# Which gathers SyncE fetches, and how the last step of a spiking recurrence is cut into pieces

## The chip, the cores and the metric

The kernel runs on one core of one Trainium2 chip. The metric is the time of one execution on the device, in microseconds. Beside it there is a profile of one execution, taken by the hardware profiler; its times are counted from the start of that execution.

The core's engines work side by side and meet at semaphores. TensorE (PE in the profile) multiplies matrices and transposes, VectorE (DVE) and ScalarE (ACT) work elementwise, GpSimd (POOL) here issues the gathers, and SyncE (SP) issues plain transfers. Transfers run on DMA engines of their own.

## The reference

A table of 100001 items with 128 values each is read for 1024 users with 50 items each. From the running mean of a user's items, normalised over the users at every step, a spiking neuron is driven; the mean of its spikes is multiplied with the whole table.

```python
emb = emb_table.at[0].set(0.0)
e = emb[seq]                                   # 1024 users x 50 steps x 128
prefix = jnp.cumsum(e, axis=1)
denom = jnp.minimum(t_idx[None, :], lengths[:, None])
uF = prefix / denom[:, :, None]
mean = uF.mean(axis=0)                         # over the users
var = uF.var(axis=0)
y = (uF - mean) * lax.rsqrt(var + BN_EPS) * gamma + beta
x_seq = jnp.moveaxis(y, 1, 0)

def step(v, x):
    v = v + (x - v) / TAU                      # TAU = 2
    spike = atan_spike(v - V_TH)               # 1 where v >= 1
    v = v - spike * V_TH
    return (v, spike)

_, spikes = lax.scan(step, v0, x_seq)          # 50 steps, one after the other
uF_out = spikes.mean(axis=0)
scores = uF_out @ emb.T                        # 1024 x 100001
```

## The kernel before

The kernel has two stages. The first is the recurrence: for every step, GpSimd gathers 1024 rows of the table, 128 rows (one "column block" of users) at a time; TensorE transposes them, adding onto the running sums `pre` in PSUM; VectorE makes `uF`, its statistics, the scale `a`, and the new `v`; ScalarE applies scale and bias. `negv` holds spike minus v of the step before, so that v = x/2 + v_old/2 - spike/2 is one instruction. The spikes are counted by TensorE in `sums`.

Some of the gathers, four of 400, are not made by GpSimd. SyncE reads the item numbers into registers and starts one transfer of 512 bytes for each row, after it has started the transfer of the first 36 blocks of the table.

```python
        for g in range(AHEAD):
            fetch(group(g), g * GROUP, GROUP)
# ...
        aside = {}
        for t0, many in ((T - 6, 4),):
            for t in range(t0, t0 + many):
                aside[t] = once.tile([P, P], F32, tag=f"aside{t}", name=f"aside_{t}")
            for p in range(P):
                _, items = nc.values_load_multi_w_load_instructions(
                    idx[p : p + 1, 0, t0 : t0 + many],
                    engines=[mybir.EngineType.SP],
                    min_val=0,
                    max_val=N - 1,
                    skip_runtime_bounds_check_because="items are rows of the table; the transfer checks its own bounds",
                )
                for j, item in enumerate(items):
                    nc.sync.dma_start(out=aside[t0 + j][p : p + 1, :], in_=table[bass.ds(item, 1), :])

        es = {}

        def gather(t):
            es[t] = gp.tile([P, B], F32, tag="e", name=f"e_{t}")
            for n in range(t in aside, NB):
                nc.gpsimd.indirect_dma_start(
                    out=es[t][:, n * P : (n + 1) * P],
                    out_offset=None,
                    in_=table,
                    in_offset=bass.IndirectOffsetOnAxis(ap=idx[:, n, t : t + 1].bitcast(U32), axis=0),
                )
```

`fetch(r, q, n)` starts the transfer of `n` blocks of 1024 table rows (512 KB each).

The body of a step. The last step (49) differs: its spikes and `negv` come first, and after the statistics TensorE does transpositions into `warm`, whose results nobody reads, until the products begin.

```python
        for t in range(T):
            last = t == T - 1
            if t + 1 < T:
                gather(t + 1)
            e = es.pop(t)
            if last:
                s = lp.tile([P, B], BF16, tag="s", name=f"s_{t - 1}")
                nc.vector.tensor_single_scalar(s, v, V_TH, ALU.is_ge)
                nc.vector.tensor_tensor(negv, s, v, ALU.subtract)
            uF = up.tile([P, B], F32, tag="uF", name=f"uF_{t}")
            bs = sp.tile([P, B // BANK, 6], F32, tag="bs", name=f"bs_{t}")
            for h, cs in enumerate(halves):
                for k in range(0, BANK, P):
                    nc.tensor.matmul(
                        pre[h][:, k : k + P],
                        lhsT=aside[t] if h == k == 0 and t in aside else e[:, h * BANK + k : h * BANK + k + P],
                        rhs=ident,
                        start=False,
                        stop=last,
                        is_transpose=True,
                        skip_group_check=True,
                    )
                nc.vector.scalar_tensor_tensor(uF[:, cs], rlen[:, cs], 1.0 / (t + 1), pre[h], ALU.max, ALU.mult)
                nc.vector.bn_stats(bs[:, h, :], uF[:, cs])
            if not last:
                correct(t + 1, l)
            else:

                counted(t - 1, s)
                count = once.tile([P, B], F32, tag="zT", name="count")
                for h, cs in enumerate(halves):
                    nc.scalar.copy(count[:, cs], sums[h])
            mv = sp.tile([P, 2], F32, tag="mv", name=f"mv_{t}")
            nc.vector.bn_aggr(mv, bs.rearrange("p h s -> p (h s)"))


            r = sp.tile([P, 1], F32, tag="r", name=f"r_{t}")
            nc.scalar.activation(r, mv[:, 1:2], AF.Sqrt, bias=eps)
            nc.scalar.activation(uF, uF, AF.Identity, bias=mv[:, 0:1], scale=-1.0)


            if t and not last:
                s = lp.tile([P, B], BF16, tag="s", name=f"s_{t - 1}")
                nc.vector.tensor_single_scalar(s, v, V_TH, ALU.is_ge)
                counted(t - 1, s)

            nc.vector.reciprocal(r, r)
            q = sp.tile([P, 1], F32, tag="q", name=f"q_{t}")
            nc.vector.tensor_mul(q, r, r)
            nc.vector.scalar_tensor_tensor(q, mv[:, 1:2], BN_EPS, q, ALU.add, ALU.mult)
            nc.vector.tensor_scalar(q, q, -0.5, 1.5, ALU.mult, ALU.add)
            a = sp.tile([P, 1], F32, tag="a", name=f"a_{t}")
            nc.vector.tensor_scalar(a, q, r, hgb[:, 0:1], ALU.mult, ALU.mult)


            def x(vt, cs):
                nc.scalar.activation(vt, uF[:, cs], AF.Identity, bias=hgb[:, 1:2], scale=a)

            def step(vt, cs):
                nc.vector.scalar_tensor_tensor(vt, negv[:, cs], -0.5, vt, ALU.mult, ALU.add)

            if not last:
                vt = vp.tile([P, B], F32, tag=f"v{t % 2}", name=f"v_{t}")
                x(vt, whole)
                if t:
                    nc.vector.tensor_tensor(negv, s, v, ALU.subtract)
                step(vt, whole)
                v = vt
                if t + 2 < T:
                    l = only(t + 2)
```

After the last step the 1024 columns are finished in three groups of 128, 512 and 384; the first gives `countA`, with which TensorE starts on the scores.

```python
        warm = vp.tile([P, HALF], F32, tag="v0", name="warm")
        for k in range(2 * KQ):
            nc.tensor.transpose(warm[:, k % KQ * P : (k % KQ + 1) * P], ident, ident)
        vC = vp.tile([P, B - BANK - P], F32, tag="v1", name="vC")
        groups = [
            (slice(0, P), pre[0][:, :P], countA),
            (slice(P, P + BANK), pre[1], countB),
            (slice(P + BANK, B), vC, countC),
        ]
        for cs, vt, _ in groups:
            x(vt, cs)
        cs, vt, first = groups[0]
        step(vt, cs)
        spiked(first, cs, vt)
        for cs, vt, _ in groups[1:]:
            step(vt, cs)
        for cs, vt, c in groups[1:]:
            spiked(c, cs, vt)


        po1 = vp.tile([P, HALF], F32, tag="v0", name="po_0_1")
        for q, (pool, tag, po) in enumerate(((gp, "e", sums), (up, "uF", [po1[:, cs] for cs in halves]))):
            o = pool.tile([P, HALF], F32, tag=tag, name=f"o_0_{q}")
            for h, cs in enumerate(halves):
                product(po[h], q, 0, h * BANK, BANK)
            for h, cs in enumerate(halves):
                if q and h:
                    nc.vector.tensor_scalar_mul(o[:, cs], po[h], 1.0 / T)
                else:
                    nc.scalar.mul(o[:, cs], po[h], 1.0 / T)
                store(0, q * HALF + h * BANK, o[:, cs])
# ... the second stage: all other products, evictions and stores
```

In the second stage the table's blocks are transposed and split into a high and a low part (`hi`, `lo`), multiplied with the counts, scaled by 1/50 on the way out of PSUM, and stored.

Of the kernel before, what the change touches and what calls it, by code (L numbers as in the profile page):

```python
# [20 lines left out]
P = 128  # L21
# [8 lines left out]
WIDTHS = [2, 2, 2, 3, 3, 3, 3] + 12 * [6] + [4, 4]  # L30
NARROW, MIDDLE = 3, 7
# [3 lines left out]
def rec_kernel(  # L35
# [125 lines left out]
    with ExitStack() as ph:  # L161
# [17 lines left out]
        for g in range(AHEAD):  # L179
            fetch(group(g), g * GROUP, GROUP)  # L180
# [4 lines left out]
        for t0, many in ((T - 6, 4),):  # L185
            for t in range(t0, t0 + many):
                aside[t] = once.tile([P, P], F32, tag=f"aside{t}", name=f"aside_{t}")
            for p in range(P):
                _, items = nc.values_load_multi_w_load_instructions(
                    idx[p : p + 1, 0, t0 : t0 + many],  # L190
                    engines=[mybir.EngineType.SP],
                    min_val=0,
                    max_val=N - 1,
                    skip_runtime_bounds_check_because="items are rows of the table; the transfer checks its own bounds",
                )
                for j, item in enumerate(items):
                    nc.sync.dma_start(out=aside[t0 + j][p : p + 1, :], in_=table[bass.ds(item, 1), :])
# [3 lines left out]
        def gather(t):  # L201
            es[t] = gp.tile([P, B], F32, tag="e", name=f"e_{t}")
            for n in range(t in aside, NB):
# [89 lines left out]

        whole = slice(0, B)
# [5 lines left out]
        for t in range(T):  # L300
# [4 lines left out]
            if last:  # L305
                s = lp.tile([P, B], BF16, tag="s", name=f"s_{t - 1}")
                nc.vector.tensor_single_scalar(s, v, V_TH, ALU.is_ge)
                nc.vector.tensor_tensor(negv, s, v, ALU.subtract)
            uF = up.tile([P, B], F32, tag="uF", name=f"uF_{t}")
            bs = sp.tile([P, B // BANK, 6], F32, tag="bs", name=f"bs_{t}")  # L310
            for h, cs in enumerate(halves):
                for k in range(0, BANK, P):
                    nc.tensor.matmul(  # L313
                        pre[h][:, k : k + P],
                        lhsT=aside[t] if h == k == 0 and t in aside else e[:, h * BANK + k : h * BANK + k + P],
# [6 lines left out]
                nc.vector.scalar_tensor_tensor(uF[:, cs], rlen[:, cs], 1.0 / (t + 1), pre[h], ALU.max, ALU.mult)  # L322
                nc.vector.bn_stats(bs[:, h, :], uF[:, cs])  # L323
            if not last:
                correct(t + 1, l)
            else:

                counted(t - 1, s)
# [8 lines left out]
            nc.scalar.activation(r, mv[:, 1:2], AF.Sqrt, bias=eps)  # L337
# [54 lines left out]
        for cs, vt, _ in groups[1:]:  # L392
            step(vt, cs)
# [119 lines left out]
```

## Time and profile before

| | |
|---|---|
| time, median of 3 runs | 1776.19 us (1770.98 to 1776.40) |
| the profiled execution | 1571.61 us, span 1569.9 us |
| TensorE | 1153.1 us busy (73%) |
| VectorE | 940.7 us (60%) |
| ScalarE | 630.6 us (40%) |
| GpSimd | 374.6 us (24%), 396 gathers of 944 ns each |
| scores written | 409.6 MB |
| table and item rows read from HBM | 77.69 MB |

The profiled execution was shorter than the timed ones; the profile is of one execution and the times are of others. Shares of the whole span mix the two stages: GpSimd's 24% lies in the first third alone, and the DMA engines, at 0.2 of their time there, are busy without a pause in the second. So the profile has to be read stage by stage. In a row of the timeline the first number is the start, the second the duration, then engine, line of the program, operation, what is written and read, shapes, and in brackets how long the engine was idle before it and what ended that.

### The profile page before, as it was taken

The numbers are of one execution on the slowest core, as the hardware profiler recorded it, in microseconds if no ns is written. First come the engines' busy times: TensorE is split into PE (matmuls) and PEld (weight loads), VectorE is DVE, ScalarE is ACT, GpSimd is POOL, SyncE is SP. The second block draws the span as 40 slices with busy tenths as digits, with TensorE's granted clock in tenths as the row PEclk, the third lists the DMA queues.
The fourth block names the chain that finished last, engine by engine and source line by source line (L and its number), as shares of the span: only waits on it lengthen the run. The fifth ranks groups of instructions, "written<-read, shape, count | busy, mean of one in ns | idle before, by whom it ended". The sixth has DMA issues, their size and how long they took to land.

```text
span 1569.9 us, 14231 instructions
## 1 busy us (share of the span) xinstructions
PE 1153.1 (73%) x4548; PEld 822.3 (52%) x4548; DVE 940.7 (60%) x1161; ACT 630.6 (40%) x700; POOL 374.6 (24%) x402
## 2 busy tenths in 40 slices
PE   4555555555556988899878788887788888788784
PEld 2222222222233766677666666666666666666563
DVE  4777777777778665576545555555555545555453
ACT  2322222222233554465444444444444444444342
POOL 6777777777775000000000000000000000000000
PEclk7555555555555999999999988999999998989998
DMA  9622222222222999999999999999999999999998
GB/s 342 245 55 53 55 54 54 54 53 54 52 53 64 399 411 420 420 393 428 425 432 427 429 428 424 418 422 424 428 413 420 415 424 429 421 423 409 394 423 354
DMA packets 54600, 488.25 MB, mean 311 GB/s; under 512 B 12443, under 2 KB 13756, under 8 KB 33276
## 3 DMA queue, kind: packets, MB, share of 16 engines
q1 hardware_dynamic: 33008, 429.03, 65.1%
q0 software_dynamic: 12672, 25.98, 6.2%
q10 hardware_dynamic: 8844, 32.33, 5.2%
q8 instruction: 36, 0.59, 0.1%
q14 instruction: 40, 0.33, 0.1%
HBM read 77.69 MB, written 409.60 MB: 310 GB/s over the span
## 4 chain that ended last, share of the span: by engine, by line
DMA 52%; POOL 17%; PE 11%; issue 9%; ACT 5%; DVE 4%; DVEq 0%; ACTq 0%; SPq 0%; POOLq 0%
DMA scores<-o 49%; POOL e L204 17%; PE po L149 9%; ACT o L473 5%; DMA e<-in_L_rec_emb_table,idx 3%; DVE o L471 2%; PE pt L119 1%; DVE bs L323 1%; DVE uF L322 0%; DVE s L343 0%; PE pre L313 0%; PE sums L281 0%; DMA idx<-in_r_seq 0%; ACT hi L141 0%; ACT pairs L141 0%
## 5 line engine op out<-in xcount | busy, mean ns | idle before, releaser
L471 DVE TENSOR_SCALAR o<-po 128x1024 f32<-128x1024 f32 x391 | 463.5, 1220 | 351.8 <-DMA scores<-o 323.4
L473 ACT ACTIVATE o<-po 128x1024 f32<-128x1024 f32 (+1 forms) x391 | 387.9, 1018 | 547.8 <-DMA scores<-o 344.9
L204 POOL DMA_INDIRECT e<-in_L_rec_emb_table,idx x396 | 373.9, 944 | 123.4 <-issue 114.6
L149 PE MATMUL po<-pairs,countB 128*128 128x512 f32 x1168 | 314.7, 415 | 67.6 <-ACT o L473 50.7
L149 PEld LDWEIGHTS po<-pairs,countB 128*128 128x128 f32 x1168 | 225.8, 198 | 132.5 <-ACT o L473 65.8
L149 PE MATMUL po<-pairs,countC 128*128 128x512 f32 x876 | 239.1, 419 | 43.6 <-ACT o L473 43.6
L313 PE MATMUL pre<-ident,e 128*128 128x128 f32 x396 | 153.1, 450 | 143.8 <-DMA e<-in_L_rec_emb_table,idx 142.2
L149 PEld LDWEIGHTS po<-pairs,countC 128*128 128x128 f32 x876 | 170.1, 200 | 89.7 <-ACT o L473 54.7
L313 PEld LDWEIGHTS pre<-ident,e 128*128 128x128 f32 x396 | 78.5, 201 | 236.1 <-DMA e<-in_L_rec_emb_table,idx 214.7
L142 DVE TENSOR_TENSOR pairs<-pt,pairs 128x1024 fp32r<-128x1024 f32 (+1 forms) x73 | 88.3, 1217 | 96.6 <-ACT pairs L141 96.5
L337 ACT ACTIVATE r<-mv,eps 128x1 f32<-128x1 f32 x50 | 14.7, 295 | 300.6 <-DVE mv L333 300.6
L322 DVE SCALAR_TENSOR_TENSOR uF<-rlen,pre 128x512 f32<-128x512 f32 x100 | 68.3, 683 | 103.8 <-PE pre L313 103.8
L119 PE MATMUL pt<-ident,rows 128*128 128x128 f32 x782 | 113.5, 293 | 8.0 <-ACT o L473 3.9
L119 PEld LDWEIGHTS pt<-ident,rows 128*128 128x128 f32 x782 | 102.6, 154 | 28.8 <-issue 10.0
L149 PE MATMUL po<-hi,countB 128*128 128x512 f32 x200 | 82.8, 414 | 18.8 <-ACT o L473 13.8
L281 PE MATMUL sums<-s,ident_h 128*128 128x512 bf16 x98 | 49.6, 608 | 60.6 <-DVE s L343 60.6
L270 PE MATMUL pre<-zT,l 128*128 128x512 f32 x100 | 78.0, 782 | 21.6 <-DVE uF L322 21.5
L149 PE MATMUL po<-lo,countB 128*128 128x512 f32 x200 | 80.4, 402 | 0.0
L141 ACT CAST pairs<-pt 128x1024 fp32r<-128x1024 f32 (+1 forms) x73 | 73.6, 1008 | 16.2 <-PE pt L119 15.9
L149 PE MATMUL po<-pairs,countA 128*128 128x512 f32 (+1 forms) x292 | 73.2, 393 | 9.1 <-ACT o L473 9.1
L149 PE MATMUL po<-hi,countC 128*128 128x512 f32 x150 | 62.7, 418 | 16.4 <-ACT o L473 16.4
L356 ACT ACTIVATE v<-uF,hgb,a 128x1024 f32<-128x1024 f32 x49 | 59.2, 1208 | 37.4 <-DVE a L352 37.4
(78 smaller groups left out, 821.1 us busy)
## 6 DMA issues: line engine op xcount, KB each, us to landing
scores<-o SPq DMA_DIRECT2D x96, 3072.0 KB
scores<-o SPq DMA_DIRECT2D x32, 1536.0 KB
rows<-in_L_rec_emb_table ACTq DMA_DIRECT2D x20, 1536.0 KB
scores<-o SPq DMA_DIRECT2D x22, 1024.0 KB
rows<-in_L_rec_emb_table SPq DMA_DIRECT2D x6, 3072.0 KB
scores<-o SPq DMA_DIRECT2D x8, 2048.0 KB
scores<-o SPq DMA_DIRECT2D x8, 1872.5 KB
aside<-in_L_rec_emb_table SPq DMA_DIRECT2D x512, 0.5 KB
```

Of the source, the lines that this page charges most:

```text
L119: nc.tensor.transpose(pt[:, k0 : k0 + kw], r[:kw, k0 : k0 + D], ident[:kw, :kw])
L141: nc.scalar.copy(vh, vp)
L142: nc.vector.tensor_tensor(vl, vp, vh.bitcast(F32), ALU.subtract)
L149: nc.tensor.matmul(po[:, :kw], lhsT=counts[n], rhs=part[:, k0 : k0 + kw], start=j == 0, stop=j == 1,)
L204: nc.gpsimd.indirect_dma_start(out=es[t][:, n * P : (n + 1) * P], out_offset=None, in_=table, in_offset=bass.IndirectOffsetOnAxis(ap=idx[: ...
L270: nc.tensor.matmul(pre[h], lhsT=l, rhs=zT[:, h * BANK : (h + 1) * BANK], start=t == 0, stop=False, skip_group_check=True,)
L281: nc.tensor.matmul(sums[h], lhsT=ident_h, rhs=s[:, h * BANK : (h + 1) * BANK], start=t == 0, stop=t == T - 2, skip_group_check=True,)
L313: nc.tensor.matmul(pre[h][:, k : k + P], lhsT=aside[t] if h == k == 0 and t in aside else e[:, h * BANK + k : h * BANK + k + P], rhs=ident ...
L322: nc.vector.scalar_tensor_tensor(uF[:, cs], rlen[:, cs], 1.0 / (t + 1), pre[h], ALU.max, ALU.mult)
L356: nc.scalar.activation(vt, uF[:, cs], AF.Identity, bias=hgb[:, 1:2], scale=a)
L471: nc.vector.tensor_scalar_mul(o[:, h0 : h0 + hw], po[:, :hw], 1.0 / T)
L473: nc.scalar.mul(o[:, h0 : h0 + hw], po[:, :hw], 1.0 / T)
```

## The change

SyncE takes six gathers instead of four: the last two column blocks of steps 46, 47 and 48, in place of the first block of steps 44 to 47. Its item numbers come from a small tile of their own, loaded early. It no longer starts the first 36 blocks of the table at once: six go first, and after every fourth partition's rows one more follows.

In the last step the pieces are the first 512 columns, then the last 384, then the 128 between. GpSimd makes the gather of those 128 last, so that little is left to do when it lands. The counting of the step before goes between the second piece and the third. `negv` of the last step is no longer one instruction ahead of `uF` but three, by the groups of the finish: the first while VectorE waits for the square root, the second after `a`, the third after `countA`. `warm` moves to the buffer of v of step 47, as v of step 48 is read longer.

In every step the refinement of the reciprocal square root is written with one instruction fewer after the square root: var + eps is made while ScalarE works.


```diff
--- before.py
+++ after.py
@@ -28,6 +28,7 @@
 AHEAD = 6
 
 WIDTHS = [2, 2, 2, 3, 3, 3, 3] + 12 * [6] + [4, 4]
+LATE = 3
 NARROW, MIDDLE = 3, 7
 
 
@@ -176,31 +177,42 @@
         gb = once.tile([P, 2], F32, tag="gb", name="gb")
         nc.sync.dma_start(out=gb[:, 0:1], in_=gamma.rearrange("(d o) -> d o", o=1))
         nc.sync.dma_start(out=gb[:, 1:2], in_=beta.rearrange("(d o) -> d o", o=1))
-        for g in range(AHEAD):
-            fetch(group(g), g * GROUP, GROUP)
+        last3 = once.tile([P, 2, 4], I32, tag="last3", name="last3")
+        late = last3.rearrange("p n t -> p (n t)")[:, : 2 * LATE].rearrange("p (n t) -> p n t", t=LATE)
+        nc.sync.dma_start(out=late, in_=seq.rearrange("(n p) t -> p n t", p=P)[:, NB - 2 :, T - 1 - LATE : T - 1])
+        tiles = [group(g) for g in range(AHEAD)]
+        fetch(tiles[0], 0, GROUP)
 
 
 
         aside = {}
-        for t0, many in ((T - 6, 4),):
-            for t in range(t0, t0 + many):
-                aside[t] = once.tile([P, P], F32, tag=f"aside{t}", name=f"aside_{t}")
-            for p in range(P):
-                _, items = nc.values_load_multi_w_load_instructions(
-                    idx[p : p + 1, 0, t0 : t0 + many],
-                    engines=[mybir.EngineType.SP],
-                    min_val=0,
-                    max_val=N - 1,
-                    skip_runtime_bounds_check_because="items are rows of the table; the transfer checks its own bounds",
-                )
-                for j, item in enumerate(items):
-                    nc.sync.dma_start(out=aside[t0 + j][p : p + 1, :], in_=table[bass.ds(item, 1), :])
+        for n in (NB - 2, NB - 1):
+            for t in range(T - 1 - LATE, T - 1):
+                aside[t, n] = once.tile([P, P], F32, tag=f"aside{n}_{t}", name=f"aside_{n}_{t}")
+        ahead = GROUP
+        for p in range(P):
+            _, items = nc.values_load_multi_w_load_instructions(
+                last3.rearrange("p n t -> p (n t)")[p : p + 1, : 2 * LATE],
+                engines=[mybir.EngineType.SP],
+                min_val=0,
+                max_val=N - 1,
+                skip_runtime_bounds_check_because="items are rows of the table; the transfer checks its own bounds",
+            )
+            for r, item in zip(aside.values(), items):
+                nc.sync.dma_start(out=r[p : p + 1, :], in_=table[bass.ds(item, 1), :])
+            if p % 4 == 3 and ahead < AHEAD * GROUP:
+                fetch(tiles[ahead // GROUP], ahead, 1)
+                ahead += 1
+        assert ahead == AHEAD * GROUP
 
         es = {}
 
         def gather(t):
             es[t] = gp.tile([P, B], F32, tag="e", name=f"e_{t}")
-            for n in range(t in aside, NB):
+            order = [n for n in range(NB) if (t, n) not in aside]
+            if t == T - 1:
+                order.append(order.pop(NB // 2))
+            for n in order:
                 nc.gpsimd.indirect_dma_start(
                     out=es[t][:, n * P : (n + 1) * P],
                     out_offset=None,
@@ -291,6 +303,12 @@
         def spiked(out, cs, v):
             nc.vector.scalar_tensor_tensor(out, v, V_TH, count[:, cs], ALU.is_ge, ALU.add)
 
+
+        thirds = [slice(0, P), slice(P, P + BANK), slice(P + BANK, B)]
+
+        def negated(cs):
+            nc.vector.tensor_tensor(negv[:, cs], s[:, cs], v[:, cs], ALU.subtract)
+
         whole = slice(0, B)
         halves = [slice(h * BANK, (h + 1) * BANK) for h in range(B // BANK)]
         v = None
@@ -305,27 +323,39 @@
             if last:
                 s = lp.tile([P, B], BF16, tag="s", name=f"s_{t - 1}")
                 nc.vector.tensor_single_scalar(s, v, V_TH, ALU.is_ge)
-                nc.vector.tensor_tensor(negv, s, v, ALU.subtract)
             uF = up.tile([P, B], F32, tag="uF", name=f"uF_{t}")
-            bs = sp.tile([P, B // BANK, 6], F32, tag="bs", name=f"bs_{t}")
-            for h, cs in enumerate(halves):
-                for k in range(0, BANK, P):
+
+
+            pieces = halves if not last else halves[:1] + [slice(B - 3 * P, B), slice(BANK, BANK + P)]
+            bs = sp.tile([P, len(pieces), 6], F32, tag="bs", name=f"bs_{t}")
+            for j, cs in enumerate(pieces):
+                h = cs.start // BANK
+                if last and j == len(pieces) - 1:
+
+                    counted(t - 1, s)
+                for c0 in range(cs.start, cs.stop, P):
+                    k = c0 - h * BANK
                     nc.tensor.matmul(
                         pre[h][:, k : k + P],
-                        lhsT=aside[t] if h == k == 0 and t in aside else e[:, h * BANK + k : h * BANK + k + P],
+                        lhsT=aside.get((t, c0 // P), e[:, c0 : c0 + P]),
                         rhs=ident,
                         start=False,
                         stop=last,
                         is_transpose=True,
                         skip_group_check=True,
                     )
-                nc.vector.scalar_tensor_tensor(uF[:, cs], rlen[:, cs], 1.0 / (t + 1), pre[h], ALU.max, ALU.mult)
-                nc.vector.bn_stats(bs[:, h, :], uF[:, cs])
+                nc.vector.scalar_tensor_tensor(
+                    uF[:, cs],
+                    rlen[:, cs],
+                    1.0 / (t + 1),
+                    pre[h][:, cs.start - h * BANK : cs.stop - h * BANK],
+                    ALU.max,
+                    ALU.mult,
+                )
+                nc.vector.bn_stats(bs[:, j, :], uF[:, cs])
             if not last:
                 correct(t + 1, l)
             else:
-
-                counted(t - 1, s)
                 count = once.tile([P, B], F32, tag="zT", name="count")
                 for h, cs in enumerate(halves):
                     nc.scalar.copy(count[:, cs], sums[h])
@@ -335,6 +365,8 @@
 
             r = sp.tile([P, 1], F32, tag="r", name=f"r_{t}")
             nc.scalar.activation(r, mv[:, 1:2], AF.Sqrt, bias=eps)
+            ve = sp.tile([P, 1], F32, tag="ve", name=f"ve_{t}")
+            nc.vector.tensor_scalar_add(ve, mv[:, 1:2], BN_EPS)
             nc.scalar.activation(uF, uF, AF.Identity, bias=mv[:, 0:1], scale=-1.0)
 
 
@@ -343,10 +375,11 @@
                 nc.vector.tensor_single_scalar(s, v, V_TH, ALU.is_ge)
                 counted(t - 1, s)
 
+            if last:
+                negated(thirds[0])
             nc.vector.reciprocal(r, r)
             q = sp.tile([P, 1], F32, tag="q", name=f"q_{t}")
-            nc.vector.tensor_mul(q, r, r)
-            nc.vector.scalar_tensor_tensor(q, mv[:, 1:2], BN_EPS, q, ALU.add, ALU.mult)
+            nc.vector.scalar_tensor_tensor(q, r, ve, r, ALU.mult, ALU.mult)
             nc.vector.tensor_scalar(q, q, -0.5, 1.5, ALU.mult, ALU.add)
             a = sp.tile([P, 1], F32, tag="a", name=f"a_{t}")
             nc.vector.tensor_scalar(a, q, r, hgb[:, 0:1], ALU.mult, ALU.mult)
@@ -362,7 +395,7 @@
                 vt = vp.tile([P, B], F32, tag=f"v{t % 2}", name=f"v_{t}")
                 x(vt, whole)
                 if t:
-                    nc.vector.tensor_tensor(negv, s, v, ALU.subtract)
+                    negated(whole)
                 step(vt, whole)
                 v = vt
                 if t + 2 < T:
@@ -375,20 +408,18 @@
 
 
 
-        warm = vp.tile([P, HALF], F32, tag="v0", name="warm")
+        warm = vp.tile([P, HALF], F32, tag="v1", name="warm")
         for k in range(2 * KQ):
             nc.tensor.transpose(warm[:, k % KQ * P : (k % KQ + 1) * P], ident, ident)
         vC = vp.tile([P, B - BANK - P], F32, tag="v1", name="vC")
-        groups = [
-            (slice(0, P), pre[0][:, :P], countA),
-            (slice(P, P + BANK), pre[1], countB),
-            (slice(P + BANK, B), vC, countC),
-        ]
+        groups = list(zip(thirds, (pre[0][:, :P], pre[1], vC), (countA, countB, countC)))
+        negated(thirds[1])
         for cs, vt, _ in groups:
             x(vt, cs)
         cs, vt, first = groups[0]
         step(vt, cs)
         spiked(first, cs, vt)
+        negated(thirds[2])
         for cs, vt, _ in groups[1:]:
             step(vt, cs)
         for cs, vt, c in groups[1:]:
```


## The prediction

> **What bounds the kernel now.** I read four views: the table of busy time by stretch of the span, the list of waits, the timeline of steps 47 to 49, and SyncE's own timeline. The stretches come first, because the kernel has two stages that share almost nothing. Columns after the stretch and its length: PE, weight load, VectorE, ScalarE, GpSimd busy us (instructions), TensorE clock, DMA share, GB/s.
>
> ```profile
> 200.00:300.00 100.00, 52.39 (x122) 23.48 (x121) 71.48 (x131) 28.81 (x41) 75.62 (x81) 0.50 0.21 54
> 500.00:507.00 7.00, 6.54 (x26) 5.35 (x27) 5.69 (x16) 5.01 (x9) 0.00 (x0) 0.59 0.00 0
> 700.00:1000.00 300.00, 254.03 (x1124) 201.54 (x1122) 162.96 (x138) 137.64 (x140) 0.00 (x0) 0.94 1.01 427
> ```
>
> Up to about 500 us is the recurrence: the DMA engines are used a fifth, GpSimd issues gathers. From 507 us the scores are written, at a DMA share of about 1. The 7 us between are the tail of step 49, in which nothing moves. The list of waits says what the first stage waits for:
>
> ```profile
> ACT o L473 <- DMA scores<-o: 344.9, 138, 5.5
> PEld pre L313 <- DMA e<-in_L_rec_emb_table,idx: 214.7, 229, 1.7
> POOL e L204 <- issue: 114.6, 376, 0.3
> ```
>
> GpSimd's own waits are "issue", 0.3 us each: nothing that it needs is late, it goes from gather to gather. The second issue starts at 5.77 us and the last at 497.64, with 394 pitches between: 1.248 us each. Eight gathers make 9.99 us a step, seven 8.74, six 7.49. The timeline shows what VectorE needs for a step, and the end:
>
> ```profile
> 480.71 0.68 DVE L322 SCALAR_TENSOR_TENSOR uF<-rlen,pre 128x512 f32<-128x512 f32 x1
> 485.75 1.23 DVE L359 SCALAR_TENSOR_TENSOR v<-negv,v 128x1024 f32<-128x1024 f32 x1 [0.21 <-ACT v L356]
> 487.60 0.69 DVE L323 BATCH_NORM_STATS2 bs<-uF 128x6 f32<-128x512 f32 x1
> ...
> 496.99 1.22 DVE L307 TENSOR_SCALAR s<-v 128x1024 bf16<-128x1024 f32 x1
> 497.64 0.94 POOL L204 DMA_INDIRECT e<-in_L_rec_emb_table,idx  x1 [0.30 <-issue]
> 498.25 1.22 DVE L308 TENSOR_TENSOR negv<-s,v 128x1024 f32<-128x1024 bf16 x1
> 499.39 0.68 DVE L322 SCALAR_TENSOR_TENSOR uF<-rlen,pre 128x512 f32<-128x512 f32 x1
> 500.26 0.47 PE L313 MATMUL pre<-ident,e 128*128 128x128 f32 x1 [0.89 <-DMA e<-in_L_rec_emb_table,idx]
> 500.77 0.69 DVE L322 SCALAR_TENSOR_TENSOR uF<-rlen,pre 128x512 f32<-128x512 f32 x1
> 502.22 0.21 DVE L333 BATCH_NORM_AGGREGATE mv<-bs 128x2 f32<-128x12 f32 x1
> 503.57 0.27 DVE L352 TENSOR_SCALAR a<-q,r,hgb 128x1 f32<-128x1 f32 x1
> 504.43 0.29 DVE L359 SCALAR_TENSOR_TENSOR pre<-negv,pre 128x128 f32<-128x128 f32 x1 [0.59 <-ACT pre L356]
> 504.76 0.29 DVE L292 SCALAR_TENSOR_TENSOR countA<-pre,count 128x128 fp32r<-128x128 f32 x1
> 505.20 0.70 PE L149 MATMUL sums<-hi,countA 128*128 128x512 f32 x1 [0.20 <-ACT pre L356]
> ```
>
> From a second-half uF to the place of the next step's second half (487.60 + 0.69 = 488.29) VectorE takes 7.6 us with hardly a gap. So a step of eight or seven gathers is set by GpSimd, and a step of six by both at once: 7.6 of VectorE against 7.49. After the last gather the chain is: transposition 500.26, uF and bn_stats of 512 columns, mv, six tiny instructions to a, the first 128 columns of the step, countA, first product at 505.20. SyncE, at last, is idle for the recurrence after this:
>
> ```profile
> 38.04 318.47 SPq L197 DMA_DIRECT2D aside<-in_L_rec_emb_table  x512
> ```
>
> **What the Trainium skill says.** "DMA: Bandwidth & Descriptors", section "SWDGE vs HWDGE vs iDMA": GpSimd computes a gather's descriptors in software, a transfer from SyncE gets them from hardware. The trace agrees on the relief: GpSimd's pitch is 1.248 us whatever SyncE does. Its section "Issuing engines are not separate DMA queues" says that all transfers run on the same 16 engines and interleave, so that another issuer saves only issue time; that is the case here, at a DMA share of 0.21. The same page, "Latency and other measured facts", gives about 600 ns as the floor of a register load from memory; the trace has 0.56 us for SyncE's. "VectorE: DVE Perf Modes", section on the SBUF-source erratum, says that an instruction pays a fixed cost beside its elements; here 1024 columns take 1.21 us and 512 take 0.69, so splitting costs about 0.15 us a cut.
>
> **The change part by part.**
>
> Gathers: six instead of four (3 steps by 2 columns, for 4 steps by 1), so 394 for 396 on GpSimd: 2 x 1.248 = 2.50 us earlier for the last landing, 497.76 in place of 500.26 (all times below are on this trace's clock).
>
> VectorE against that. Steps 46, 47 and 48 now have six gathers. ve adds one tiny instruction between mv and s, which has to wait for mv (about 0.30 us), and the q chain loses one (0.195): 7.7 us a step. The last gather of step 45 lands 2 x 1.248 later than now, at 465.3, its second uF at 465.8. Then VectorE: 465.8 + 7.7 = 473.5, 481.2, 488.9 for the second uF of steps 46 to 48; gathers alone would give 473.3, 480.8, 488.3. VectorE is the later one by 0.6. From a second uF to the end of v is 496.96 - 490.69 = 6.27 in this trace, with ve 6.4: 495.3. s: 496.5. negv is gone from here, so uF and bn of the first half (1.38) end at 497.95, of the 384 columns (two of about 0.54) at 499.03. The last gather's columns are landed at 497.76, but their transposition writes the PSUM tile that the 384-column uF reads and so waits for it: to about 499.05. So the whole 2.5 us of gathers is not waited for any more; VectorE's own work ends at the same point. uF and bn of 128 columns, 0.3 each: mv at about 499.75, against 502.22: 2.5 us gained. This is not 2.5 for the gathers plus 0.8 for the short piece (four instructions of 0.69 against 0.3): without the negv moved out, VectorE would have eaten most of both.
>
> After mv. ve and the first negv (128 columns, 0.29) lie in the 0.36 us in which VectorE waits for the square root: reciprocal 0.15 later. q one fewer: 0.195 earlier. a ends at 501.35 (503.84 now). The second negv, 512 columns, 0.68, then stands before the first step, which waited 0.59 for ScalarE anyway: 0.1 lost. countA 502.7 (505.05 now), first product 502.8: 2.4 us earlier. Third negv, 384 columns, 0.55, goes before countB: 505.15, where TensorE wants it at 504.95: 0.3 us of stall, once, and two evictions are due then. Nothing of this is repeated.
>
> SyncE must have brought 768 rows. One partition now takes 2.29 us (load 0.62, then 0.46 and three of 0.405); with six rows 3.1, times 128 is 397 us, plus 30 table pieces of about 0.5 us, plus a start at 6.5 and some waits behind the pieces (eight lanes, 3.2 us apart): done at 420 to 450 us. Step 46 reads the first of them at about 472. It fits, by 20 to 50 us.
>
> The table's first 18 MB used to go in a burst in the first 50 us (387 GB/s) and are now spread over 400 us. GpSimd's pitch was the same in the burst and after it, so nothing is to be gained there, nor lost.
>
> Sum: the first store and everything behind it moves 2.0 to 2.5 us earlier; the write stage is a row of stores at a DMA share of 1, so the end moves as much. 1776.2 - 2.4 = 1773.8, that is 0.14%.
>
> **Rivals.** (1) SyncE is late with the rows. For it: 50% more rows, pieces of 512 KB in the same queue, and a lane's wait for its last transfer. Each us late beyond 470 is a us of the end. It would need 50 us of stalls; the burst at the start cost some 20 in this trace. Result 1776 to 1800. (2) VectorE takes the gain: if ve and the smaller pieces cost 0.2 us more each than I gave them, three tied steps and the tail give back 1.5 us, and the time is 1775.5; nobody could tell it from before. (3) The gain is larger: if the recurrence stays on GpSimd's pitch (VectorE's 7.6 hides below 7.49 because some of its instructions overlap), 2.5 + 0.8 + 0.2 for the tail: 1772.7. (4) The moved start changes how stores and table loads meet in the write stage. The stage ran at 410 to 428 GB/s throughout, so there is little to shift, but a few us either way are possible.
>
> **Range and chances.** The profiled execution took 1571.61 us where the timed ones took 1776; no view shows where those 205 us lie. If they lie in the write stage, the gain is as above; if the gathers were slower by 0.5 us each, two of them would be worth 3.5 us. Both end within 5 us of the same place. The three times before span 5.4 us, more than the effect, which is most of the range: 1765 to 1779. Two per cent is 35 us. No part of the change is that big except rows arriving very late; 1% faster, 2% slower, the rest within.
>
> **What would show it.** After, GpSimd has 394 gathers at the same 1.248; SyncE's rows end before 450 us; the second uF of steps 46 to 48 follow each other by 7.6 to 7.7 us with no wait for a gather; mv of step 49 stands some 2.5 us earlier, the first store at about 504.4 for 506.78; the span is 1567 to 1568. I am wrong if a transposition of step 46 waits for a row of SyncE, if the pitch of gathers grows in the 400 us in which table pieces now pass, or if the write stage has another length than 1063 us.

## The result and the profile after

The changed kernel takes 1914.09 us (median of 5, 1911.41 to 1917.10) where the kernel before takes 1776.19: 1.078 times as long, 95% interval 1.075 to 1.080. The prediction was 1773.8 within 1765 to 1779, and the reason is the first of its rivals, SyncE late with its rows. It had put that at 1776 to 1800 us, and had given two chances in a hundred to a time over 2% slower.

The page of the changed kernel, GpSimd's row of the slices (each a fortieth of the span, busy tenths) and the chain that ended last, by engine:

```profile
POOL 6666766666630000010000000000000000000000
DMA 40%; SPq 14%; PE 8%; issue 7%; ACT 4%; DVE 3%; DVEq 0%; ACTq 0%
```

The chain on the page of before:

```profile
DMA 52%; POOL 17%; PE 11%; issue 9%; ACT 5%; DVE 4%; DVEq 0%; ACTq 0%; SPq 0%; POOLq 0%
```

GpSimd works through twelve slices, stands still for five and makes its last gathers in the eighteenth. On the chain SyncE's queue (SPq) has taken GpSimd's place: the end now goes back through SyncE's rows.

The list of waits of the changed kernel (who waits for whom, total us, times, longest) has lines that have no counterpart before:

```profile
PEld pre L338 <- DMA aside<-in_L_rec_emb_table: 268.5, 2, 267.5
POOL e L216 <- PE pre L338: 270.4, 3, 267.0
DVE uF L347 <- remote: 148.8, 28, 11.6
POOL e L216 <- remote: 66.0, 20, 4.6
```

TensorE waits 267.5 us, once, for a row that SyncE fetches; GpSimd stands still as long, as its next buffer is not free. The two lines with "remote" are another matter: VectorE and GpSimd wait 215 us in all for semaphore updates that come long after any instruction that could have made them, so that the view can't put them down to anyone. The first profile of before has no such wait. The table of stretches (columns as before) says where the time lies:

```profile
200.00:300.00 100.00, 35.09 (x103) 21.29 (x101) 59.59 (x106) 24.08 (x34) 65.66 (x70) 0.52 0.24 63
600.00:700.00 100.00, 0.00 (x0) 0.00 (x0) 0.00 (x0) 0.00 (x0) 0.00 (x0) 0.50 0.12 38
900.00:1900.00 1000.00, 835.94 (x3658) 656.47 (x3656) 542.21 (x461) 449.91 (x459) 0.00 (x0) 0.94 1.00 420
```

From 200 to 300 us GpSimd has 70 instructions where the first profile of before had 81; from 600 to 700 nothing computes at all; the write stage runs at 420 GB/s as it did. It begins at 846.15 us, and 1909.6 - 846.2 = 1063 us, the same as before. Everything is in the first stage. SyncE's own instructions in two stretches of this kernel, 306 to 326 us, while gathers run, and 612 to 632 us, while nothing else does (duration in ns min/median/max):

```profile
L202 SPq FUSED_REGOPS  x11: 3/221/1397, 306.0 to 325.7; - x11
L202 SPq MOVE aside<-in_L_rec_emb_table x11: 3/29/722, 306.9 to 325.8; - x11
L202 SPq DMA_DIRECT2D aside<-in_L_rec_emb_table x11: 2/225/712, 306.9 to 325.9; - x11
...
L202 SPq DMA_DIRECT2D aside<-in_L_rec_emb_table x32: 224/228/269, 612.0 to 630.8; - x32
L202 SPq FUSED_REGOPS  x31: 37/37/37, 612.2 to 630.7; - x31
L202 SPq MOVE aside<-in_L_rec_emb_table x31: 29/29/29, 612.3 to 630.8; - x31
```

11 rows in 20 us against 32. A move between registers, which waits for no transfer, takes up to 722 ns beside the gathers and 29 ns alone; the register operations before it (FUSED_REGOPS) have a median of 221 ns against 37. So SyncE is not waiting for a transfer; it crawls. Single durations are to be taken with care here, as some moves are noted with 3 ns, less than a free one takes; the number of rows in a stretch is the sounder measure.

### The profile page after: what moved, and what is told of

It is laid out like the page before. It is cut to its first block, busy times and chain, and to the rows that moved or that the text cites. A ratio compares the mean times of both kernels' runs of the same rounds, so it can differ in the third digit from the quotient of the medians.

```text
span 1909.6 us, 15034 instructions
## 1 busy us (share of the span) xinstructions
PE 1109.0 (58%) x4548; PEld 831.9 (44%) x4548; DVE 945.6 (50%) x1165; ACT 631.1 (33%) x700; POOL 372.6 (20%) x400
## 4 chain that ended last, share of the span: by engine, by line
DMA 40%; SPq 14%; PE 8%; issue 7%; ACT 4%; DVE 3%; DVEq 0%; ACTq 0%
DMA scores<-o 40%; SPq L202 10%; PE po L150 8%; SPq L194 4%; ACT o L504 4%; DVE o L502 2%; SPq L98 0%; PE pt L120 0%; DVE bs L355 0%; DVE uF L347 0%; ACT pairs L142 0%; DVE v L392 0%; ACT v L389 0%; DVE s L375 0%; DVE pairs L143 0%
## 5 line engine op out<-in xcount | busy, mean ns | idle before, releaser
L150 PE MATMUL po<-pairs,countB 128*128 128x512 f32 x1168 | 310.8, 411 | 64.3 <-ACT o L504 48.2
L347 DVE SCALAR_TENSOR_TENSOR uF<-rlen,pre 128x512 f32<-128x512 f32 (+1 forms) x101 | 68.1, 674 | 436.3 <-PE pre L338 266.4
L150 PE MATMUL po<-pairs,countC 128*128 128x512 f32 x876 | 244.6, 426 | 49.0 <-ACT o L504 49.0
L282 PE MATMUL pre<-zT,l 128*128 128x512 f32 x100 | 72.0, 722 | 260.6 <-DVE uF L347 210.6
L282 PEld LDWEIGHTS pre<-zT,l 128*128 128x128 f32 x100 | 26.8, 269 | 300.5 <-issue 210.3
L338 PE MATMUL pre<-ident,e 128*128 128x128 f32 x394 | 97.1, 420 | 7.1 <-DMA e<-in_L_rec_emb_table,idx 5.6
L338 PEld LDWEIGHTS pre<-ident,e 128*128 128x128 f32 x394 | 85.0, 226 | 33.6 <-issue 21.8
```

The lines of the kernel that those rows point to most:

```text
L150: nc.tensor.matmul(po[:, :kw], lhsT=counts[n], rhs=part[:, k0 : k0 + kw], start=j == 0, stop=j == 1,)
L282: nc.tensor.matmul(pre[h], lhsT=l, rhs=zT[:, h * BANK : (h + 1) * BANK], start=t == 0, stop=False, skip_group_check=True,)
L338: nc.tensor.matmul(pre[h][:, k : k + P], lhsT=aside.get((t, c0 // P), e[:, c0 : c0 + P]), rhs=ident, start=False, stop=last, is_transpose= ...
```

## The experiments

**Was the first profile of before the kernel that was timed?** The first run is the kernel before itself, for a trace beside its own timed runs; the next runs take the rows away or undo the spread of the table blocks. A session, below, is a set of runs made together on one chip, with the kernel before among them.

> The kernel before, unchanged, for its trace beside its own timed runs. Theory A (SyncE runs slowly while GpSimd gathers, and the rows that it fetches come late, in the timed runs of before as well): about 1776 us; SyncE's 512 rows end well after 356 us, near 600 us, GpSimd waits about 200 us for step 44, the write stage is 1063 us as in the first profile. Theory B (only the change makes SyncE slow; the timed runs of before are long for another reason): about 1776 us with rows that end near 356 us and a write stage of some 1268 us.

Measured: 1781.87 us. SyncE's timeline of this run, and from its list of waits the one at step 44:

```profile
38.47 619.01 SPq L197 DMA_DIRECT2D aside<-in_L_rec_emb_table  x512
```

```profile
PE pre L313 <- DMA aside<-in_L_rec_emb_table: 132.8, 1, 132.8
```

512 rows took 619 us here and 318 in the first profile, and TensorE waited 132.8 us for them. The first store is at 714.2 us, against 506.8; the write stage has 1064 us. So the 205 us that the prediction could not place, between the profiled execution and the timed ones, lie in the first stage, and 133 of them are this wait for SyncE's rows; the next run shows what the others are. Theory A holds in its main point (it had put the wait at about 200 us), B falls. The kernel before took 1571 us in the one execution of the first profile and in one session below, and 1776 to 1782 in all eight other sessions; each comparison here is with the kernel before in its own session.

No rows at all by SyncE, first from the kernel before, then from the changed kernel:

```diff
-        for t0, many in ((T - 6, 4),):
-            ...                                   # tiles, register loads, 512 transfers
         # aside stays empty: GpSimd makes all 400 gathers
```

> The kernel before with all 400 gathers made by GpSimd and none by SyncE. Theory A: the first stage is GpSimd's pitch alone, 400 x 1.248 us, so 5 us above the first profile: about 1577 us, 11% faster than before. Theory B: 5 us above the timed 1776: about 1781 us.

Measured: 1652.63 us, 0.926 times before (0.923 to 0.929). Expected were 1577: taking the rows away brings 129 us, not 200. The rest does not come from SyncE's rows. The timeline of this run around step 17:

```profile
206.73 0.47 PE L300 MATMUL pre<-ident,e 128*128 128x128 f32 x1 [0.75 <-DMA e<-in_L_rec_emb_table,idx]
...
213.60 0.69 DVE L309 SCALAR_TENSOR_TENSOR uF<-rlen,pre 128x512 f32<-128x512 f32 x1 [7.08 <-remote]
...
219.23 0.69 DVE L309 SCALAR_TENSOR_TENSOR uF<-rlen,pre 128x512 f32<-128x512 f32 x1 [4.22 <-remote]
219.47 0.94 POOL L191 DMA_INDIRECT e<-in_L_rec_emb_table,idx  x1 [4.32 <-remote]
```

The transposition at 206.73 is the eighth and last of its step. VectorE reads the first four only at 213.60 and the others at 219.23, and GpSimd, which waits for the transpositions before it fills a buffer again, starts at 219.47. After that two steps run at VectorE's 7.49 us, and then it comes again. The last of the 400 gathers starts at 565.7 us, one in 1.41 us, though each still follows the last in 1.25 us wherever GpSimd isn't stopped.

> The changed kernel with all 400 gathers made by GpSimd, the table's first blocks fetched at once, and its last step with three pieces and negv by thirds kept. Theory A: about 1574 to 1576 us, some 1 to 2.5 us below the kernel before without rows, which is the worth of the last step's part. Theory B, or if the last step were what cost the 138 us: 1900 us or more.

Measured: 1648.46 us, 0.923 (0.920 to 0.927). The last step cost nothing; against the run before it is 4.2 us less by the medians, in traces with this stutter, so not much can be read from that. Repeated in another session:

> The changed kernel without rows by SyncE, again. Limit absent: 400 gathers by 1.248 and the shorter last step: 1574 to 1576 us, 6 to 7 us above the changed kernel, which is what six gathers are worth. Limit present: 1648 us as before.

Measured: 1647.31 us, 0.927 (0.924 to 0.930).

The changed kernel with the table's blocks in one burst again:

```diff
-        fetch(tiles[0], 0, GROUP)
+        for g in range(AHEAD):
+            fetch(tiles[g], g * GROUP, GROUP)
...
-            if p % 4 == 3 and ahead < AHEAD * GROUP:
-                fetch(tiles[ahead // GROUP], ahead, 1)
-                ahead += 1
```

> The changed kernel with the first 36 table blocks fetched at once as before, and six gathers' rows by SyncE after them. Theory A (number of rows, not the spread table blocks): rows are as late as in the changed kernel, 1890 to 1940 us. Theory C (the table pieces between the rows are what makes SyncE slow): rows at 3.1 us a partition end near 460 us and the time is near that of before or below, 1570 to 1780 us.

Measured: 1922.71 us, 1.078 (1.074 to 1.081); the last row at 825.6 us against 814.7. Theory C falls: the pieces between the rows don't make SyncE slow.

**What makes SyncE crawl?** First, fewer rows by the changed kernel, then half of the gathers, then GpSimd slowed down without leaving anything out.

```diff
-LATE = 3
+LATE = 1
```

> The changed kernel with SyncE making two gathers (256 rows, for step 48) instead of six. Theory D (beside gathers SyncE issues some 60 rows in 100 us, whatever their number, and the loss is what is left to issue when GpSimd has to stop): 256 rows end near 430 us, before step 48 at about 560, nothing waits for them, and the time is that of the changed kernel without rows less two gathers: about 1645 us. Rival E (rows beside gathers slow the gathers in proportion): between 1648 and 1914, near 1735 us.

Measured: 1650.78 us, 0.927 (0.925 to 0.929). The 256 rows ended at 517.5 us, later than expected, but nothing waited for them. That speaks for D and against E: rows that are ready in time cost next to nothing, and the loss is what is left to issue when GpSimd must stop. It also gains nothing over no rows at all: two gathers fewer don't show.

```diff
-            for n in range(t in aside, NB):
+            for n in range(t in aside, NB // 2):
...                                               # and the transpositions' operands
```

> The kernel before with only the first four column blocks of each step gathered (the other four are transposed from the same rows, so half of the gathers is left out), SyncE's 512 rows kept. GpSimd's mean pitch is then set by the step of VectorE, 7.5 us for 4 gathers. Theory F (SyncE crawls because GpSimd issues faster than some path takes it, one gather in 1.42 us): no crawl, rows at their 2.3 us for four end before 400 us, first stage some 385 to 400 us, time 1450 to 1465 us. Rival G (SyncE crawls beside any gathers): rows still at 60 in 100 us, first stage 500 us or more, 1570 to 1640 us.

Measured: 1481.67 us, 0.832 (0.830 to 0.833), with half of the gathers left out. SyncE's timeline:

```profile
36.78 328.33 SPq L197 DMA_DIRECT2D aside<-in_L_rec_emb_table  x512
```

The crawl is gone: 328 us for what took 619. The time is 17 us over the range that theory F gave: at VectorE's pace step 44 needs the rows at 346.5 us already, and TensorE waited 18.4 us there for the last one, of 365. But half of the work was left out too, so the next runs leave it in:

```diff
+        pad = once.tile([P, 128], F32, tag="pad", name="pad")     # then 1, 304, 250 columns
...
                 nc.gpsimd.indirect_dma_start(...)
+                nc.gpsimd.memset(pad, 0.0)
```

> The kernel before with a memset of 128 columns on GpSimd after each gather, nothing left out: GpSimd's pitch becomes about 1.5 us. Theory F: a slower GpSimd makes the kernel faster: no crawl, rows end near 360 us, 396 gathers by 1.5 make a first stage of about 605 us, time 1665 us. Rival G: the rows come as late as before or later: 1780 us or more.

> The same with a memset of one column, GpSimd's pitch about 1.35 us, still under 1.42. Theory F: still over the limit, so the crawl stays though it is shorter: 1700 to 1780 us. If the limit is not at 1.42 but anywhere above 1.248: no crawl, 396 by 1.35 is 535 us, time 1608 us. Rival G: 1780 us or more.

Measured: 1774.08 us, 0.996 (0.994 to 0.998), and 1778.07 us, 1.000 (0.999 to 1.002). Both missed their purpose: the pitch of the gathers became 1.335 us and stayed at 1.25, because a memset, 0.22 us with 128 columns, mostly takes the place of the 0.3 us between two gathers. Both stay below 1.42 and both crawl (64 and 59 rows from 200 to 300 us), which F allows and G too.

> The kernel before with a memset of 304 columns after each gather, so that GpSimd's pitch is about 1.5 us (the memset of 128 columns made it 1.33 only). Theory F (limit at one gather in 1.42 us): no crawl of SyncE, its 512 rows end near 360 us, the first stage is 396 by 1.5 and a tail, some 605 us, the time about 1670 us: less work per time on GpSimd, and 6% faster than before. Rival G (any gathers make SyncE crawl): 1780 us or more.

Measured: 1664.72 us, 0.936 (0.934 to 0.938), pitch 1.48 us. Nothing of the kernel was removed, GpSimd was given 304 columns of useless work 396 times, and the kernel became 6.4% faster, beside a kernel before at 1778.14 us. SyncE's timeline, and the stretch from 200 to 300 us (GpSimd's count includes the memsets):

```profile
36.53 335.55 SPq L197 DMA_DIRECT2D aside<-in_L_rec_emb_table  x512
```

```profile
200.00:300.00 100.00, 44.42 (x103) 19.40 (x101) 61.44 (x112) 24.50 (x35) 88.93 (x135) 1.00 0.18 46
```

512 rows in 336 us, and no stutter: a full step takes 11.9 us, eight times 1.48, and no wait is put down to "remote" any more (235 us for VectorE and GpSimd in the kernel before). G falls. F holds so far, but for its number (see below).

> The changed kernel with the same memset. Theory F: 768 rows at 3.1 us a partition and 30 table pieces end between 430 and 480 us, before step 46 at some 560, nothing waits, time about 1665 us, a few us below the paced kernel before, as the prediction reckoned without the crawl. Rival G: 1914 us or more.

Measured: 1661.23 us, 0.934 (0.933 to 0.936): 3.5 us less than the paced kernel before. The rows ended at 507.8 us, 28 later than expected, still ahead of their use: nothing waits for them.

Is the limit one of rows or of gathers? Half as many rows in each gather:

```diff
-                    out=es[t][:, n * P : (n + 1) * P],
+                    out=es[t][: P // 2, n * P : (n + 1) * P],
...
-                    in_offset=bass.IndirectOffsetOnAxis(ap=idx[:, n, t : t + 1].bitcast(U32), axis=0),
+                    in_offset=bass.IndirectOffsetOnAxis(ap=idx[: P // 2, n, t : t + 1].bitcast(U32), axis=0),
...                                               # and transpositions of 64 columns
```

> The kernel before with gathers of 64 rows instead of 128, as many gathers as before (half of the users are left out of the sums, so half of the gathered rows), SyncE's 512 rows kept. GpSimd issues up to 8 gathers in VectorE's 7.5 us. If the limit is one of rows (128 in 1.42 us, so 90 in a us): 8 x 64 in 7.5 us is 68 in a us, no crawl, SyncE's rows end near 360 us, time 1450 to 1480 us. If the limit is one of gathers (one in 1.42 us): 11.3 us a step and crawl as before, time 1750 us or more.

Measured: 1747.66 us, 0.983 (0.981 to 0.984), with half of the users left out. The stretch from 200 to 300 us, and SyncE in it:

```profile
200.00:300.00 100.00, 33.27 (x110) 15.86 (x109) 65.23 (x123) 26.58 (x37) 64.17 (x72) 1.00 0.11 24
```

```profile
200.05 97.60 SPq L197 DMA_DIRECT2D aside<-in_L_rec_emb_table  x58
```

Still 72 instructions of GpSimd in 100 us, and 58 rows by SyncE. The last of 396 gathers of 64 rows starts at 566.7 us, as the last of 400 of 128 did at 565.7. So neither the rows nor the bytes are limited. The gathers' DMA queue, in the unchanged kernel before and in this run (packets, MB, share of 16 engines):

```profile
q0 software_dynamic: 12672, 25.98, 5.0%
q0 software_dynamic: 12672, 13.00, 3.3%
```

The bytes are halved, the number of packets is not: 32 for each gather in both. It is a limit of gathers or of something that each gather has a fixed number of, such as its packets; these runs don't tell them apart.

**How sharp is it?** The changed kernel with 250 columns, a pitch of 1.437 us, in two sessions.

> The changed kernel with a memset of 250 columns after each gather, GpSimd's pitch about 1.435 us, just above 1.42. Theory H (the limit is one gather in 1.42 us on average, and nothing is lost above it): no crawl, 394 by 1.435 and a tail make a first stage of about 580 us, time 1643 us, below every kernel so far. If the limit isn't sharp, or SyncE's own transfers count against it: SyncE crawls again in part and the time is 1660 to 1780 us.

> The changed kernel with the memset of 250 columns, again. Limit absent: 1643 us as in the last run, where the slower pitch only costs. Limit present: 1643 us too, since a pitch of 1.435 is above the limit of 1.42; if the limit isn't sharp, 1660 to 1780 us.

Measured: 1643.28 us first, but beside a kernel before that took 1571.21 in that session (1.046, 1.044 to 1.048), so this run says nothing of the limit; the slower pitch only costs there. These runs were made on the chip (number 3) on which the kernel before took 1781.74 us in the first session of these experiments, so the chip alone does not decide. Then 1776.82 us beside 1778.22 (0.999, 0.997 to 1.001). SyncE's transfers of rows from 200 to 300 us, in the first session and in the second:

```profile
L202 SPq DMA_DIRECT2D aside<-in_L_rec_emb_table x164: 224/228/272, 199.8 to 300.0; - x164
L202 SPq DMA_DIRECT2D aside<-in_L_rec_emb_table x101: 2/223/756, 200.0 to 299.7; - x101
```

The same kernel has 164 rows in one and 101 in the other; at a pitch of 1.48 us it had 159, limit present. In the second session the gathers kept their pitch, with no wait put down to "remote", until they had to stop at 559 us for the last row, which came at 690.1 us. So there is no sharp threshold at 1.42: at 1.44 the gathers are no longer delayed, and SyncE still is. That the gathers have precedence and SyncE gets what they leave is a reading of this, not shown. The expected 1643 was wrong for a session with the limit.

**The changed kernel where the limit is absent.** Four runs of the kernel of the result, unchanged:

> The changed kernel, unchanged, again, because the kernel before took 1571 us beside the last run and 1776 to 1782 us beside all others. Theory F with its limit absent (before at 1571 here): no crawl, rows end between 420 and 450 us, the prediction's own account holds, 2.4 us below before: 1568 to 1570 us. With the limit present (before at 1776 or so): 1914 us as measured, rows end near 815 us.

> The changed kernel once more, to meet a session in which the kernel before takes 1571 us. Limit absent: rows end between 420 and 450 us, 1568 to 1570 us, 2.4 us below before. Limit present: 1914 us.

> The same again, for the same question. Limit absent: 1568 to 1570 us, 2.4 us below before. Limit present: 1914 us.

> The same again, for the same question. Limit absent: 1568 to 1570 us, 2.4 us below before. Limit present: 1914 us.

Measured: 1910.30, 1912.29, 1916.33 and 1915.73 us, beside a kernel before at 1776 to 1782: ratios 1.074 to 1.077. None met a session of the other kind, so the change was never measured there.

## Why the prediction was wrong

**SyncE "done at 420 to 450 us".** This is the step that failed: the prediction's own sign of being wrong, a transposition of step 46 that waits for a row of SyncE, is what came. It took SyncE's 2.29 us for four rows from the one profile at hand and scaled it to six. Its rival (1) named the event by luck more than by reasoning: the causes that it gave were table pieces in the queue and a wait of SyncE for its own transfers, and the run with the blocks in one burst shows that the pieces don't matter. In the sessions with the limit SyncE makes some 60 rows in 100 us while GpSimd gathers, and some 165 when GpSimd has stopped. The changed kernel needs all 768 of its rows; GpSimd can go on to about 550 us, by then some 340 are issued, and the others need 260 us more. That agrees with the 267.5 us of TensorE's wait. Before it was 132.8 us for 512 rows. From there the sum: the last row comes at 814.7 in place of 657.3 us, 157 later; after it the changed kernel needs 31.5 us to its first store and the kernel before 56.9. 157 - 25 is 132, the two traces' first stores are 846.2 and 714.2, and the times differ by 138.

The term was also mis-sized in itself. The load of six item numbers takes 0.99 us (0.56 for four), and the prediction's sum left the load as it was for four; with these 0.43 us more a partition takes 3.5 us alone, not 3.1. In the session without the limit, the rows of the changed kernel with 250 columns of memset ended at 482 us, beyond 450. In the first profile step 46 has its last transposition at 471.5 us. So, as an estimate from these two, step 46 would have waited some 10 us there, four times the 2.4 that were to be gained. No run shows it.

**"GpSimd's pitch is 1.248 us whatever SyncE does."** The pitch of a single gather is; the mean, up to the wait for SyncE's rows, was 1.40 to 1.44 us in every trace of a session with the limit in which GpSimd was neither paced nor short of work. The prediction read the waits called "issue" as proof that GpSimd was bound by itself, and in that profile it was.

**"No view shows where those 205 us lie."** They were the warning, and the prediction used them for the width of a range of 14 us. 75 of them are the limit on gathers (the kernel before without rows by SyncE has its first store at 586.5 us, against 506.8 in the first profile, less 5 for four more gathers) and 133 are the wait for rows: 208 together. The prediction had asked what gathers slower by 0.5 us each would do; they were slower by some 0.18 on the average. That the rows come late in the kernel before as well it did not ask. An execution 12% shorter than the times isn't a picture of them, and the page of before should not have been read as one.

**What held.** The write stage did not change its length (1063 to 1064 us in every kernel run). The spread table blocks changed nothing in the ratio (1.078 with and without). VectorE's step with ve is 7.58 us, 7.7 predicted. The last step, in the changed kernel's timeline:

```profile
837.19 1.22 DVE L325 TENSOR_SCALAR s<-v 128x1024 bf16<-128x1024 f32 x1
841.41 0.23 DVE L363 BATCH_NORM_AGGREGATE mv<-bs 128x2 f32<-128x18 f32 x1
844.31 0.77 PE L150 MATMUL sums<-hi,countA 128*128 128x512 f32 x1 [0.17 <-ACT pre L389]
846.15 3.58 SPq L159 DMA_DIRECT2D scores<-o  x5
```

From s to mv 4.22 us in place of 5.23, 1.0 shorter; from mv to the first product 2.90 in place of 2.98; from there to the first store 1.84 in place of 1.58, since the first two products took 0.77 and 0.62 us instead of 0.70 and 0.39; countB was there in time, so the stall of 0.3 us that the prediction put there did not come. Where 304 columns of memset took the stops away, the whole change brought 3.5 us (1664.72 against 1661.23): two gathers by 1.48 are 3.0 of them, and the predicted 2.4 is of this size. So the parts were reckoned well enough, and the one thing they all rested on, that SyncE has time, was taken from an execution that was not like the others.

Of the versions run, the one to keep where the limit is present is the changed kernel without rows by SyncE: 1647 to 1648 us, 0.923 to 0.927 of before. With two gathers by SyncE it took 1650.78, which is no better. Where it is absent, it wasn't run.

**What stays open.** Which path the limit is on, and why it is present in one session and not in another, the runs don't tell. It does not count rows or bytes; it delays the semaphores between TensorE, VectorE and GpSimd as well as SyncE's register instructions. The traces of the kernels that run against it hold fewer semaphore records (4,357 to 5,621 landings of transfers where the first profile has 10,645 and the paced kernel of the session without it 11,531; the two kernels at a pitch of 1.48 us have 8,451 and 8,045). The loss is all in the first stage: after the first store it is 3,116 in the first profile and in the unchanged kernel before of a session with the limit, before it 7,529 and 1,674. It looks as if the reports of events shared the path; that is an argument, not a proof. Whether the recording itself takes part wasn't tried, and it matters: every timed execution here has a span and a clock from its recording, so no run shows the limit without one. Nor was a gather's count of packets or semaphore updates varied.

## What to carry to other kernels

Compare the span of a profile with the timed runs before reading anything else; if they differ by more than the effect in question, take another trace until they agree. Work that is moved to an engine with idle time has to be sized at that engine's rate in company, measured beside what runs there, and the instructions to look at are the cheapest: here register moves of up to 0.7 us in place of 0.03 gave SyncE's crawl away. And when a producer runs against a limit that others share, slowing it down can be the gain: 304 columns of memset after each gather made the kernel before 6% faster, where the limit was present.

## What the runs showed of the hardware

GpSimd's gathers go out every 1.25 us, but in eight of ten sessions (the first profile counted as one) no more than one in 1.40 to 1.44 us gets through on the average, with 128 rows or with 64. At this limit SyncE's register moves take up to 1.4 us in place of 0.03, and VectorE starts 6 and 12 us after TensorE's last transposition of a step. At a pitch of 1.48 us SyncE has 152 to 159 rows in 100 us, at 1.44 about 100, at the limit about 60, and 164 at 1.44 where the limit is absent. A load of registers from memory took SyncE 0.56 us for four values and 0.99 us for six.
